# Two recurrences of a metaformer on two groups of 256 columns instead of four of 128

## The chip, the cores and the metric

The kernel runs on one core of one Trainium2 chip. The metric is device time in microseconds of one execution. Before the change the median of three runs is 1061.53 us (1059.64 to 1063.08). All data are 32-bit floats.

## The reference, cut to what matters

The network is two layers. In each, a token mixer (an attention block in layer 0, a filtered convolution with up- and down-sampling in layer 1) is followed by a recurrent feed-forward part, and the two recurrent parts are what the change is about. `x` has 4 batches of 32 tokens, each an image of 128 rows by 128 columns. The recurrent part sees every image row as one time step with 128 features, over 128 sequences (4 batches x 32 tokens). What is computed is:

```python
def _L0_ffn_ref(x, W, V, gamma, beta):      # _L1_ffn_ref is the same
    Wx = jnp.einsum('bti,hi->bth', x, W)
    flat = Wx.reshape(B * T, H)
    mean = jnp.mean(flat, axis=0)
    var = jnp.var(flat, axis=0)
    Wx = ((flat - mean) * jax.lax.rsqrt(var + BN_EPS) * gamma + beta).reshape(B, T, H)
    Vt = V.T

    def step(yt, wx_t):
        yt = jax.nn.sigmoid(wx_t + yt @ Vt)
        return (yt, yt)
    y0 = jnp.zeros((B, H), dtype=Wx.dtype)
    _, ys = jax.lax.scan(step, y0, jnp.swapaxes(Wx, 0, 1))
    return jnp.swapaxes(ys, 0, 1)
```

The sequence of a batch runs through all its tokens' rows, 32 x 128 = 4096 steps, each of which needs the state that the step before left. The result is added to the input of the part.

## The kernel before, in words

**How the long sequence becomes short ones.** The constants are `P = 128`, `NB = 4` batches, `NT = 32` tokens, `LEN = 32`, `WARM = 12` and `QS = P // LEN = 4`. Each image of 128 rows is cut into 4 segments of 32 rows, and all 32 x 4 images run at once. A segment doesn't know the state with which it begins. So each starts 12 rows early from a guess of 0.5 (the warm-up), and the state it has reached by then is used as the true one. After the main pass of 32 rows, `check` compares every segment's true last state with the warm-up's state of its follower. If any pair differs by over 4e-6 in absolute terms, the whole network is run again by a serial version (`sequential`); the runs here don't take that path.

**One step.** The products `W x` of a layer lie in `WX`, a view `[128 features, 4 groups of 8 tokens, 128 rows, 32]` of the tile `WXY`; the 32 is 8 tokens x 4 batches. `step(q, dst, prev, h)` (L1708) does one row `h` of one segment `q`, 128 columns (4 groups x 32 images): a product with `V` on PE into a PSUM bank of the segment's own, `ps_scan` (L1712); the combine with the row of `WX`, scaled by the normalisation, on DVE in place in PSUM (L1713); and the sigmoid on ACT into `dst` (L1714). A product is two passes on PE, so two LDWEIGHTS and two MATMUL instructions.

**Who waits for whom.** Inside a segment the three steps form a chain: the product of row i+1 needs the sigmoid of row i. The four segments are independent of each other, and their steps are traced in turn, segment by segment inside a row. `scan` (L1692) runs 12 warm-up rows and then 32 main rows this way, 44 x 4 = 176 steps per layer and 352 in all. At the end of the warm-up, the state of the last segment (`last`) is copied to the next token's first segment, `G[:, 0]`, shifted by four columns (L1729); the start of the very first token is zero (the memset in L1703).

**The two calls.** In the first layer `f0.scan()` writes each main row's state over its own row of `WX`; the convolution then reads it from there through `rows` (L1762), four PE transposes into `ps_y` for each token and an addition on DVE (L1796). In the second layer `f1.scan(output)` puts each row's state in a tile `y` of its own, two buffers for each segment, and after the steps of row i calls `output(i - 1)` (L1930): four PE transposes of the row before (L1937), one DVE addition of 512 columns to the image rows (L1938), and after every second row four stores of 128 KB on SyncE's queue.

**What sets the order.** Nobody writes the order of the engines by hand here: a scheduler orders the traced instructions by the order in which they were traced and by when their operands and buffers are ready. It also adds the waits. The mixers ahead of the recurrence have their order written out (`MIXERS`, `in_order`), which stays as it is.

**What lies around.** Ahead of the first recurrence, the last products of layer 0 go into `WX`; then the normalisation's scale and shift `s` are made by DVE and POOL (L1695 to L1700). After it comes the convolution, then the products of layer 1, the second recurrence with its output, and the checks.

Of the kernel before, what the change touches and what calls it, by code (L numbers as in the profile page):

```python
# [26 lines left out]
F32 = mybir.dt.float32  # L27
AF = mybir.ActivationFunctionType
ALU = mybir.AluOpType
# [3 lines left out]
P = 128  # L33
NB, NT = 4, 32
# [9 lines left out]
LEN, WARM = 32, 12  # L44
QS = P // LEN
# [149 lines left out]
def _network(  # L195
# [14 lines left out]
    nc = tc.nc  # L210
    mm = nc.tensor.matmul
    tt = nc.vector.tensor_tensor
    stt = nc.vector.scalar_tensor_tensor
# [4 lines left out]
    first = l0.enter_context(tc.tile_pool(name="first", bufs=1))  # L218
# [7 lines left out]
    WX = WXY[:, : 4 * P * TP * NB].rearrange("p (o h n) -> p o h n", o=4, h=P)  # L226
# [43 lines left out]
    def sm(shape, tag):  # L270
        return small.tile(shape, F32, tag=tag, name=tag)


    def rsqrt(o, v, eps, n):

        e = sm([P, NG], "rs_e")[:, :n]
        nc.vector.tensor_scalar_add(e, v, eps)  # L277
        nc.gpsimd.tensor_tensor(o, e, neg_half[:, :n], ALU.pow)  # L278
# [199 lines left out]
    def big(name):  # L478
        return psb.tile([P, 512], F32, tag="big", name=name)
# [233 lines left out]
    with (  # L713
# [168 lines left out]
        p = big("ps_s4")[:, :NB]  # L882
# [23 lines left out]
        for b in range(NB):  # L906
            q = slice(32 * b, 32 * b + 32)
            nc.scalar.copy(gram[q, :], pg[q, 32 * (b % 2) : 32 * (b % 2) + 32])
        p = big("ps_sl")[:, :NT]
# [20 lines left out]
        p = big("ps_pt").rearrange("p (g n) -> p g n", g=4)  # L930
# [17 lines left out]
        for b in range(NB):  # L948
            q = slice(32 * b, 32 * b + 32)
# [52 lines left out]
    with (  # L1002
# [3 lines left out]
        ys = [psy.tile([P, 8, 2 * KW], F32, name=f"ps_y{k}") for k in range(4)]  # L1006
        for g in range(4):
            for x_ in range(2):
# [13 lines left out]
                for k in range(4):  # L1022
                    r, half = divmod(k, 2)
                    m = slice(2 * KW * half, 2 * KW * (half + 1))

                    for b in range(NB):
                        c = slice(32 * b, 32 * b + 32)
                        i = mm(ys[k][c], PTs[:, 1 if (x_ == 1 and r == 0) else 0, g, c],  # L1028
                               df[b][:, r ^ x_, :, m], start=(g == 0 and x_ == 0), stop=(g == 3 and x_ == 1))
                        if k + b > 0:  # L1030
                            tc.keep_in_program_order(i)
        for k in range(4):
            r, half = divmod(k, 2)
            dst = YT[:, r, 16 * half : 16 * half + 16, :KW].rearrange("p (j k) w -> p k j w", k=8)
# [8 lines left out]
    with (  # L1043
# [9 lines left out]
        def one(name):  # L1053
            return np_.tile([P, 1], F32, name=name)
# [6 lines left out]
        def besides(n):  # L1061
# [3 lines left out]
        var, v0, r1, s, a, e1, q1, sv, s0 = (  # L1065
            one(k) for k in ("var", "v0", "r1", "s", "a", "e1", "q1", "sv", "s0"))
# [38 lines left out]
        p = ps3.tile([P, 1], F32, tag="e2", name="ps_e2")  # L1105
# [24 lines left out]
        for v, dst in ((a, aB), (r1, r1B)):  # L1130
            d = np_.tile([P, P], F32, tag="dg", name="dg")
            ts(d, ident, v, None, ALU.mult)
            p = ps3.tile([P, P], F32, tag="dg", name="ps_dg")
# [4 lines left out]
        p = ps3.tile([P, NT], F32, tag="dq", name="ps_dq")  # L1138
# [7 lines left out]
    with (  # L1146
# [16 lines left out]
        chunks = NT // TM  # L1163
        Z, SQ, Fz, G, gB, xin = {}, {}, {}, {}, {}, {}

# [12 lines left out]
        last = chunks - 1  # L1178

        def here(d, c, pool_, shape, tag):  # L1180
            if c not in d:
                d[c] = pool_.tile(shape, F32, tag=tag, name=tag)
            return d[c]
# [117 lines left out]
        def PG(c, k):  # L1301

            here(G, c, m2, [P, TM, 3, KH], "G3")
            g1, g2 = (m1.tile([P, TM, KH], F32, tag=t, name=t) for t in ("g1", "g2"))
# [3 lines left out]
            pool(g2, wi, Fz[c][:, i], ALU.mult)  # L1308
            pool(G[c][:, :, int(k)], g1, g2, o)

# [42 lines left out]
        def M4b(c, k):  # L1353
            Gc = G[c][:, :, 1:3]
            tt(Gc, Gc, vec["al"].unsqueeze(2).unsqueeze(3).broadcast_to([P, TM, 2, KH]), ALU.mult)
            stt(Gc, Y3[:, 1:3, :, of_tokens(c)].rearrange("p r k t -> p t r k"), scalar("attn_norm_g"), Gc,
                ALU.mult, ALU.add)

        def M4c(c, k):
            tt(G[c][:, :, 1, 16], G[c][:, :, 1, 16], vec["de"], ALU.add)  # L1360
            ts(G[c][:, :, 0], G[c][:, :, 2], -1.0, None, ALU.mult)

# [119 lines left out]
        with in_order():  # L1482
            for piece in MIXERS.split():
                name, c = piece.split(".")
                work = shared if inputs is None else shared | features
                f = max((n for n in shared | features if name.startswith(n)), key=len)
# [174 lines left out]
    def parallel():  # L1661
# [9 lines left out]
        xtp = ctx.enter_context(tc.tile_pool(name="xtp", bufs=1))  # L1671
        wk = ctx.enter_context(tc.tile_pool(name="wk", bufs=2))
# [6 lines left out]
        rest = WXY[:, 4 * P * TP * NB :]  # L1679
        guess = xtp.tile([P, NT * NB], F32, name="guess")  # L1680
        nc.gpsimd.memset(guess, 0.5)

        class Recurrence(Inputs):
# [8 lines left out]
            def scan(self, after=None):  # L1692

                mv = xtp.tile([P, 2], F32, name=f"mv{self.layer}")
                nc.vector.bn_aggr(mv, self.stats.rearrange("p t s -> p (t s)"))  # L1695
                s = xtp.tile([P, 2], F32, name=f"bs{self.layer}")
                rsqrt(s[:, 0:1], mv[:, 1:2], 1e-5, 1)
                tt(s[:, 0:1], s[:, 0:1], self.gamma, ALU.mult)
                stt(s[:, 1:2], mv[:, 0:1], -1.0, s[:, 0:1], ALU.mult, ALU.mult)
                tt(s[:, 1:2], s[:, 1:2], self.beta, ALU.add)  # L1700

                G = rest[:, 1024 : 1024 + QS * P].rearrange("p (q n) -> p q n", q=QS)
                nc.gpsimd.memset(G[:, 0, 0:NB], 0.0)  # L1703
                last = xtp.tile([P, NT * NB], F32, name="last")
                ys = {}
                with tc.tile_pool(name="ps_s", bufs=1, space=PSUM) as ps_s:

                    def step(q, dst, prev, h):  # L1708

                        p = ps_s.tile([P, 512], F32, tag=f"s{q}", name=f"ps_scan{q}")[:, :P]  # L1710
                        p4 = p.rearrange("p (o n) -> p o n", o=4)
                        mm(p4, self.t[:, 1, :], prev, start=True, stop=True)  # L1712
                        stt(p4, WX[:, :, h, :], s[:, 0:1], p4, ALU.mult, ALU.add)  # L1713
                        nc.scalar.activation(dst, p4, AF.Sigmoid, bias=s[:, 1:2])  # L1714
                        return dst

                    def tokens(v):
                        return v.rearrange("p (o n) -> p o n", o=4)

                    prev = [tokens(guess)] * QS  # L1720
                    for k in range(WARM):
                        for q in range(QS):

                            if k == WARM - 1:
                                dst = G[:, q] if q else last
                            else:
                                dst = wk.tile([P, NT * NB], F32, tag=f"yw{q}", name=f"yw{q}")
                            prev[q] = step(q, tokens(dst), prev[q], (q * LEN - WARM + k) % P)
                    nc.vector.tensor_copy(G[:, 0, NB:], last[:, : (NT - 1) * NB])  # L1729
                    prev[0] = tokens(G[:, 0])  # L1730
                    for i in range(LEN):
                        for q in range(QS):
                            h = q * LEN + i
                            if after is None:
                                y = WX[:, :, h, :]
                            else:
                                y = wk.tile([P, NT * NB], F32, tag=f"y{q}", name=f"y{q}")
                                ys[q, i] = y
                                y = tokens(y)
                            prev[q] = step(q, y, prev[q], h)  # L1740
                        if after is not None and i > 0:
                            after(i - 1, [ys.pop((q, i - 1)) for q in range(QS)])
                    if after is not None:
                        after(LEN - 1, [ys.pop((q, LEN - 1)) for q in range(QS)])
                self.ends = last, G, prev

            def check(self):
# [33 lines left out]
        with (  # L1781
# [106 lines left out]
            for n in sizes:  # L1888
                last = 2 * t0 - 4
# [7 lines left out]
            for n in sizes[::-1]:  # L1897
                last = 2 * (t0 + n - 1) + 5
# [50 lines left out]
        with tc.tile_pool(name="ps_c", bufs=1, space=PSUM) as ps_c:  # L1949
            p = ps_c.tile([1, 4], F32, name="ps_ok")  # L1950
            mm(p, ones_col, ok, start=True, stop=True)
            n = sm([1, 1], "n_ok")
# [113 lines left out]
```

## Time and profile before

| what | value |
|---|---|
| median of three runs | 1061.53 us |
| the profiled execution, own time | 1060.68 us |
| its span in the profile | 1058.9 us |
| mean granted TensorE clock | 0.947 |
| first recurrence, first combine to last row's first combine | 505.77 to 563.55 us |
| second recurrence, the same | 978.36 to 1046.69 us |
| its main pass begins | 996.24 us |
| combines (L1713), DVE | 352 x 360 ns, 102.2 us |
| products (L1712), PE | two passes each, median 275 ns a pass |
| sigmoids (L1714), ACT | 352, about 363 ns each |

A row of the profile's group table gives the line, the engine and the operation, what is written and read, the shapes as partitions x elements, the count, the total busy time and the mean of one in ns, then the idle time just before and who ended it. A row of the timeline gives the start in us, the length of the merged group, and in brackets the engine's idle time before it and the releaser. PEld is the loading of weights, PE the product itself. DVE and ACT instructions overlap at their edges, so four of 355 ns can take 1.13 us together.

### The profile page before, as it was taken

The page shows a single profiled execution, that of the slowest core. Times are in us where ns is not written, and L with a number is a line of the kernel's source. Part 1 is how long each engine was busy: PE and PEld are TensorE (multiplying, and loading weights), DVE is VectorE, ACT ScalarE, POOL GpSimd, SP SyncE. Part 2 cuts the span into 40 slices and gives each one's busy share as a digit, 9 for nine tenths or more (in the row PEclk, how much of TensorE's full clock was granted, in tenths as well). Part 3 has the DMA queues.
Part 4 walks back from the last instruction along what each step waited for, and adds up shares of the span by engine and source line. Part 5 has one row for each costly group of instructions (what it writes and reads, how often), then busy time and mean ns, then how long its engine had stood idle before and what let it go on. Part 6 is the DMA issues. An engine that isn't in the chain of part 4 may idle for free.

```text
span 1058.9 us, 18079 instructions
## 1 busy us (share of the span) xinstructions
PE 948.9 (90%) x6398; PEld 680.2 (64%) x6398; DVE 775.9 (73%) x2512; ACT 666.6 (63%) x1605; POOL 167.7 (16%) x291
## 2 busy tenths in 40 slices
PE   3999779966889998987898999999999999998996
PEld 2565455655655556543785777777777777775884
DVE  5996387784588899988888656666657566556997
ACT  3767355664637789978784545565546465655864
POOL 1000000010343535552000111111120202010000
PEclk9999989996668899999998999999999999999898
DMA  9723000001011111210000000000100000104644
GB/s 230 174 37 74 1 1 1 1 1 40 2 41 40 41 42 41 61 41 1 1 1 1 20 22 21 20 21 21 31 20 21 20 21 21 30 21 135 227 162 138
DMA packets 68965, 48.83 MB, mean 46 GB/s; under 512 B 4417, under 2 KB 63809, under 8 KB 68801
## 3 DMA queue, kind: packets, MB, share of 16 engines
q1 hardware_dynamic: 68529, 47.31, 15.5%
q8 instruction: 53, 0.87, 0.4%
q0 software_dynamic: 288, 0.01, 0.2%
q10 hardware_dynamic: 48, 0.26, 0.1%
q14 instruction: 47, 0.39, 0.1%
HBM read 30.68 MB, written 16.88 MB: 45 GB/s over the span
## 4 chain that ended last, share of the span: by engine, by line
PE 55%; DVE 23%; ACT 11%; POOL 6%; issue 3%; DMA 1%; SPq 0%; POOLq 0%; ACTq 0%; DVEq 0%
PE ps_up L1854 8%; PE ps_scan L1712 7%; PE ps_dn L1866 7%; PE ps_dn L1875 3%; PE ps_up L1843 3%; DVE XA L1382 3%; PE ps_wx L362 3%; PE ps_st L1224 3%; PE ps_st L765 3%; PE ps_y L1028 2%; DVE XA L1381 2%; PE ps_inv L397 2%; PE pm L970 2%; POOL c_r L278 2%; DVE ps_scan L1713 2%
## 5 line engine op out<-in xcount | busy, mean ns | idle before, releaser
L1857 DVE SCALAR_TENSOR_TENSOR U<-ps_up,above 128x512 f32<-128x512 f32 x128 | 86.7, 690 | 89.9 <-ACT above L1856 89.8
L1854 PE MATMUL ps_up<-q,WXY 128*128 128x512 f32 x256 | 124.0, 606 | 6.0 <-ACT q L1846 6.0
L1866 PEld LDWEIGHTS ps_dn<-WXY,U 128*128 128x128 f32 x1024 | 124.4, 192 | 3.3
L1866 PE MATMUL ps_dn<-WXY,U 128*128 128x128 f32 x1024 | 124.6, 275 | 0.0
L1713 DVE SCALAR_TENSOR_TENSOR ps_scan<-WXY,bs,ps_scan 128x128 f32<-128x128 f32 x352 | 102.2, 360 | 11.4 <-PE ps_scan L1712 10.0
L1856 ACT ACTIVATE above<-ps_up 128x512 f32<-128x512 f32 x128 | 74.4, 596 | 24.6 <-PE ps_up L1854 24.6
L1868 ACT COPY q<-ps_dn 128x512 f32<-128x512 f32 x64 | 37.5, 586 | 71.9 <-PE ps_dn L1866 71.9
L362 PE MATMUL ps_wx<-xt,wvt 128*128 128x512 f32 x128 | 69.0, 625 | 6.3 <-ACT WXY L369 4.0
L1843 PEld LDWEIGHTS ps_up<-WXY,XN 128*128 128x128 f32 x256 | 49.1, 192 | 34.8 <-issue 15.9
L1854 PEld LDWEIGHTS ps_up<-q,WXY 128*128 128x128 f32 x256 | 44.0, 193 | 38.9 <-issue 23.9
L278 POOL TENSOR_TENSOR f_r<-rs_e,neg_half 128x16 f32<-128x16 f32 (+2 forms) x10 | 23.9, 2394 | 278.4 <-DVE rs_e L277 278.4
L1843 PE MATMUL ps_up<-WXY,XN 128*128 128x256 f32 x256 | 66.6, 383 | 0.5 <-DVE XN L1813 0.5
L1875 PE MATMUL ps_dn<-q,WXY 128*128 128x256 f32 x256 | 66.0, 380 | 0.0
L765 PE MATMUL ps_st<-cst,XA 128*128 128x130 f32 x256 | 44.2, 312 | 15.0 <-ACT XA L748 12.0
L1218 ACT ACTIVATE Z<-Z,k,aB 128x128 f32<-128x128 f32 x128 | 51.3, 483 | 9.8 <-DVE Z L1213 9.8
L1875 PEld LDWEIGHTS ps_dn<-q,WXY 128*128 128x128 f32 x256 | 46.1, 190 | 16.4 <-issue 12.0
L1381 DVE SCALAR_TENSOR_TENSOR XA<-ps_inv,r1B,xin 128x128 f32<-128x128 f32 x128 | 44.1, 344 | 13.2 <-PE ps_inv L1374 13.2
L765 PEld LDWEIGHTS ps_st<-cst,XA 128*128 128x128 f32 x256 | 35.6, 208 | 28.2 <-ACT XA L748 13.1
L369 ACT COPY WXY<-ps_wx 128x512 f32<-128x512 f32 x60 | 35.0, 583 | 29.1 <-DVE bn L365 27.8
L1439 ACT ACTIVATE xn<-XA,f_o,f_r 128x128 f32<-128x128 f32 x120 | 50.4, 487 | 2.2 <-DVE f_o L1421 2.2
L412 PE MATMUL ps_inv<-invq,cst 64*128 64x512 f32 x128 | 44.7, 723 | 5.6 <-ACT invq L403 3.3
L1815 ACT ACTIVATE XN<-XA,c_o,c_r 128x128 f32<-128x128 f32 x64 | 28.8, 490 | 32.3 <-DVE c_o L1804 26.3
(425 smaller groups left out, 2143.5 us busy)
## 6 DMA issues: line engine op xcount, KB each, us to landing
XA<-in_x_dram SPq DMA_DIRECT2D x16, 512.0 KB, 7.1
xin<-in_x_dram SPq DMA_DIRECT2D x32, 256.0 KB, 3.3
turned<-XA SPq DMA_DIRECT2D x32, 256.0 KB, 2.3
XA<-turned SPq DMA_DIRECT2D x8, 1024.0 KB, 15.2
out_dram<-res SPq DMA_DIRECT2D x64, 128.0 KB, 2.1
WXY<-dd SPq DMA_DIRECT2D x4, 544.0 KB, 10.7
WXY<-md SPq DMA_DIRECT2D x4, 144.0 KB, 5.3
WXY<-m1d SPq DMA_DIRECT2D x1, 544.0 KB, 11.1
```

The source lines that it names most:

```text
L362: mm(self.held[t], self.t[:, 0, :], xt, start=True, stop=True)
L765: mm(p[:, i, :], XA[:, b, t0 + j + i, :], cst[:, C_E : C_E + 130], start=True, stop=True)
L1218: nc.scalar.activation(z, z, AF.Gelu, bias=k1, scale=aB[:, j : j + 1])
L1381: stt(a, p2[c, b][:, i], r1B[:, j : j + 1], xin[c, b - b % 2][:, b % 2, i], ALU.mult, ALU.add)
L1712: mm(p4, self.t[:, 1, :], prev, start=True, stop=True)
L1713: stt(p4, WX[:, :, h, :], s[:, 0:1], p4, ALU.mult, ALU.add)
L1843: mm(p[:, b, :], XN[u // 2][:, (u % 2) * H2 + b, :], UR.rearrange("p r q -> p (r q)"), start=True, stop=True)
L1854: mm(p, UC[:, s, :], q, start=True, stop=True)
L1856: nc.scalar.activation(above, p, AF.Relu, scale=1.0 - SLOPE)
L1857: stt(U[:, s], p, SLOPE, above, ALU.mult, ALU.add)
L1866: mm(p[:, r, b, :], U[:, s, b, r * P : (r + 1) * P], DC[:, s, :], start=(s == 0), stop=(s == 1))
L1875: mm(p, DR[:, r, :], q[:, r], start=(r == 0), stop=(r == 1))
```

## The change

A step now takes all four segments at once, for half of the tokens: the two groups are `j = 0` (token groups 0 and 1) and `j = 1` (token groups 2 and 3), each 2 x 4 x 32 = 256 columns. Both layers, warm-up and main pass, use the same form. So a row has two products, two combines and two sigmoids of 256 columns in place of four of each of 128.

The warm-up is turned by one place to make this possible. All segments read the row `LEN - WARM + k` of their own segment, and the state that segment q reaches is the beginning of segment q+1; the last warm-up row therefore writes into `ends[:, 1:]`, which is `G[1:]` followed by `last`. `last` moves from a tile of its own to a slice of `WXY` behind `G`. The copy into `G[:, 0]` stands where it stood; `G` is now read by both groups. The states of the warm-up and of the second layer's main pass lie in one tile `y` of 4 x 128 columns with two buffers, in which the halves of the tokens alternate: a group is 4 runs of 64 columns. `output` and `check` get the same values as views of these tiles.

```diff
-                    def step(q, dst, prev, h):
-                        p = ps_s.tile([P, 512], F32, tag=f"s{q}", name=f"ps_scan{q}")[:, :P]
-                        p4 = p.rearrange("p (o n) -> p o n", o=4)
-                        mm(p4, self.t[:, 1, :], prev, start=True, stop=True)
-                        stt(p4, WX[:, :, h, :], s[:, 0:1], p4, ALU.mult, ALU.add)
-                        nc.scalar.activation(dst, p4, AF.Sigmoid, bias=s[:, 1:2])
-                        return dst
+                    def step(dst, prev, i):
+                        for j in range(2):
+                            p = ps_s.tile([P, 512], F32, tag=f"s{j}", name=f"ps_scan{j}")[:, : 2 * P]
+                            p4 = p.rearrange("p (o q n) -> p o q n", o=2, q=QS)
+                            mm(p4, self.t[:, 1, :], prev(j), start=True, stop=True)
+                            v = p.rearrange("p (m n) -> p m n", n=32)
+                            stt(v, rows_in[:, i, 2 * QS * j : 2 * QS * (j + 1)], s[:, 0:1], v, ALU.mult, ALU.add)
+                            nc.scalar.activation(dst(j), p4, AF.Sigmoid, bias=s[:, 1:2])
...
                     for k in range(WARM):
-                        for q in range(QS):
...
-                            prev[q] = step(q, tokens(dst), prev[q], (q * LEN - WARM + k) % P)
+                        dst = images(ends[:, 1:] if k == WARM - 1 else wk.tile([P, QS, P], F32, tag="y", name="y"))
+                        step(dst, prev, LEN - WARM + k)
+                        prev = dst
                     nc.vector.tensor_copy(G[:, 0, NB:], last[:, : (NT - 1) * NB])
-                    prev[0] = tokens(G[:, 0])
+                    prev = images(G)
                     for i in range(LEN):
-                        for q in range(QS):
...
-                            prev[q] = step(q, y, prev[q], h)
+                        y = None if after is None else wk.tile([P, QS, P], F32, tag="y", name="y")
+                        dst = at_row(i) if after is None else images(y)
+                        step(dst, prev, i)
                         if after is not None and i > 0:
-                            after(i - 1, [ys.pop((q, i - 1)) for q in range(QS)])
+                            after(i - 1, [y0[:, q] for q in range(QS)])
+                        prev, y0 = dst, y
```

The new helpers choose the columns of a group: `half` takes 4 runs of 64 out of 4 images of 128, `at_row` takes 2 x 4 x 32 out of `WX`, and `first` spreads the guess over the segments.

```diff
+                ends = rest[:, 1024 : 1024 + (QS + 1) * P].rearrange("p (q n) -> p q n", n=P)
+                G, last = ends[:, :QS], ends[:, QS]
...
+                rows_in = WX.rearrange("p o (q i) n -> p i (o q) n", q=QS)
...
+                def half(v, j):
+                    return v.rearrange("p q (o n) -> p o q n", o=4)[:, 2 * j : 2 * j + 2]
...
+                    def at_row(i):
+                        return lambda j: WX.rearrange("p o (q i) n -> p i o q n", q=QS)[:, i, 2 * j : 2 * j + 2]
+
+                    def first(j):
+                        return tokens(guess)[:, 2 * j : 2 * j + 2].unsqueeze(2).broadcast_to([P, 2, QS, 32])
```

## The prediction

> **What bounds the kernel now.** I read the page first, then the windows of the two recurrences, then the timeline of a few rows, then the waits. The page shows an execution in which PE looks full and the combine of the recurrence (L1713) is the costliest vector group:
>
> ```profile
> span 1058.9 us, 18079 instructions
> PE 948.9 (90%) x6398; PEld 680.2 (64%) x6398; DVE 775.9 (73%) x2512; ACT 666.6 (63%) x1605; POOL 167.7 (16%) x291
> ...
> L1713 DVE SCALAR_TENSOR_TENSOR ps_scan<-WXY,bs,ps_scan 128x128 f32<-128x128 f32 x352 | 102.2, 360 | 11.4 <-PE ps_scan L1712 10.0
> ```
>
> The change touches only the two recurrences, so I read those stretches. The windows' columns are busy times of PE, PEld, DVE, ACT, POOL, then granted clock, DMA share, GB/s:
>
> ```profile
> 489.00:500.00 11.00, 7.17 (x29) 3.23 (x28) 10.00 (x37) 9.16 (x20) 1.66 (x2) 1.00 0.00 1
> 521.00:567.00 46.00, 41.83 (x267) 35.34 (x266) 39.22 (x139) 37.62 (x132) 0.10 (x1) 1.00 0.00 1
> 980.00:985.00 5.00, 5.00 (x26) 5.00 (x25) 4.11 (x12) 3.90 (x12) 0.00 (x0) 0.50 1.05 397
> 996.00:1049.00 53.00, 51.38 (x384) 43.46 (x383) 52.53 (x161) 36.98 (x129) 0.00 (x0) 1.00 0.41 141
> ```
>
> The second row is the first recurrence's main pass: no engine is full. The fourth is the second recurrence's: DVE works 52.53 of 53 us. The timeline shows why they differ. One row of the first recurrence:
>
> ```profile
> 523.43 1.13 DVE L1713 SCALAR_TENSOR_TENSOR ps_scan<-WXY,bs,ps_scan 128x128 f32<-128x128 f32 x4 [0.21 <-PE ps_scan L1712]
> 523.82 1.14 ACT L1714 ACTIVATE WXY<-ps_scan,bs 128x128 f32<-128x128 f32 x4 [0.20 <-DVE ps_scan L1713]
> 524.24 1.07 PEld L1712 LDWEIGHTS ps_scan<-WXY,wvt 128*128 128x128 f32 x8 [0.27 <-ACT WXY L1714]
> 524.76 1.13 DVE L1713 SCALAR_TENSOR_TENSOR ps_scan<-WXY,bs,ps_scan 128x128 f32<-128x128 f32 x4 [0.21 <-PE ps_scan L1712]
> ```
>
> Four segments pass in a convoy. The lead one goes DVE to ACT in 0.39 us, ACT to PE in 0.42, PE to the next DVE in 0.52: together 1.33 us, exactly the row's period, and every engine idles 0.20 to 0.27 us before the lead. So a row here costs the **latency of one chain**, not work: DVE's four combines take 1.13 us, the period is 1.33. In the second recurrence's main pass DVE also has the output addition:
>
> ```profile
> 1001.07 1.12 DVE L1713 SCALAR_TENSOR_TENSOR ps_scan<-WXY,bs,ps_scan 128x128 f32<-128x128 f32 x4
> 1002.10 0.68 DVE L1938 TENSOR_TENSOR res<-XA,ps_out 128x512 f32<-128x512 f32 x1
> 1002.70 1.13 DVE L1713 SCALAR_TENSOR_TENSOR ps_scan<-WXY,bs,ps_scan 128x128 f32<-128x128 f32 x4
> ```
>
> Here the row is 1002.70 - 1001.07 = 1.63 us = 1.03 for four combines + 0.60 for the addition: **DVE work** bounds it, above the 1.33 us latency. The waits (total us, times, longest) agree: DVE waits for PE 43 times in the first recurrence,
>
> ```profile
> DVE ps_scan L1713 <- PE ps_scan L1712: 9.0, 43, 0.3
> ```
>
> and in the second's main stretch twice, while ACT waits for DVE in every row:
>
> ```profile
> ACT y L1714 <- DVE ps_scan L1713: 15.3, 32, 0.6
> ...
> DVE ps_scan L1713 <- PE ps_scan L1712: 0.5, 2, 0.3
> ```
>
> [...] This trace: 411 ns at 256 columns and 704 at 512 (rows below), 1.14 ns an element; 683 at 512 in L1796 gives 1.06. [...] Trace: 262 ns at 130 columns, 368 at 256, 0.84 per column. [...] the sigmoid of 128 columns took 362. [...] Here a 128-column pass of L1712 has a median of 275 ns and a 256-column one a mean of 383, so 0.84 ns a column[...], and each product is issued as two passes; I take the measurement, and about 107 ns per pass of 128.
>
> ```profile
> L1843 PE MATMUL ps_up<-WXY,XN 128*128 128x256 f32 x256 | 66.6, 383 | 0.5 <-DVE XN L1813 0.5
> ...
> L1877 DVE TENSOR_TENSOR XA<-XA,ps_dn 128x256 f32<-128x256 f32 x64 | 26.3, 411 | 3.7 <-PE ps_dn L1875 1.9
> L1938 DVE TENSOR_TENSOR res<-XA,ps_out 128x512 f32<-128x512 f32 x32 | 22.5, 704 | 0.0
> ...
> L1236 ACT COPY Fz<-ps_pf 128x256 f32<-128x256 f32 x8 | 2.9, 368 | 5.4 <-PE ps_pf L384 5.3
> ...
> L769 ACT COPY A<-ps_st 128x130 f32<-128x130 f32 x8 | 2.1, 262 | 0.3 <-PE ps_st L765 0.3
> ```
>
> **The change, part by part.**
>
> *Two instructions of 256 columns for four of 128.* Work falls. On DVE one combine follows another after 0.26 us ((1.13 - 0.355)/3), so a row goes from 1.03 to 2 x (0.26 + 0.133) = 0.79 us; ACT likewise to 2 x (0.26 + 0.107) = 0.73. PE streams the same columns. But each chain gets longer, because no engine starts before the one ahead has finished its whole instruction (ACT starts 0.39 after a 0.355 us combine). The lead chain's growth: DVE +133 ns, ACT +107 ns, PE two passes of +107 = +213 ns, in all **+0.453 us**. The row becomes 1.335 + 0.453 = **1.788 us**, against 0.79 us of DVE and 0.73 of ACT work: latency-bound again, the halves following each other by about 0.43 us (PE's own time for a product).
>
> *First recurrence.* The lead combines of its 44 rows run from 505.77 to 563.55: 43 intervals, 57.78 us. One interval is special: the step from warm-up to main takes 1.60, since the copy of `last` into `G` (L1729) stands ahead of segment 0. After, both halves read the copied image, and the copy shifts by four columns across the halves, so it needs both sigmoids: 0.43 lag + 0.22 copy + 0.09 hand-overs = 0.74 extra where 0.27 was. Sum: 43 x 1.788 + 0.74 = 77.6, +19.8 us. The last chain trails the lead by 0.43 rather than 3 x 0.26 = 0.78: -0.35. **+19.5 us.**
>
> *Second recurrence, warm-up.* It runs from 978.36 to 996.24, 17.88 us. Here the clock was 0.50 for about 6.8 us (window means 0.84, 0.50 and 0.98 over 975 to 990), with 12 combines in 5 us, so 1.67 us a row: 0.33 over the full-clock row, three passes' worth (one weight load and two products of 107 ns). After, that streaming is 0.107 + 0.427 = 0.53, and a half-clock row 1.788 + 0.53 = 2.32. So 6.8/2.32 = 2.9 rows, then 9.1 x 1.788 = 16.2, plus 0.74: 23.8 us. **+5.9 us.** I keep the same half-clock time[...].
>
> *Second recurrence, main.* 31 intervals took 1046.69 - 996.24 = 50.45. DVE work is now 0.79 + 0.60 = 1.39, below the latency; PE has 0.86 of products and 4 x 0.11 of transposes, 1.3. The addition must sit between the second half's combine (free 0.82 us after the lead starts) and the next lead at 1.788: 0.97 us of room for 0.60. The transposes of the row before follow the second product in PE's queue and end before the lead's next product. So 31 x 1.788 = 55.4, +5.0, less 0.26 of shorter trail. **+4.7 us.**
>
> *The rest at nothing, together.* The row order is the same, `y` keeps two buffers, memset, check and DMAs are as before: the output stores move 8.4 MB in 57 rather than 52 us, and POOL has one memset. Were the stores' cover gone, each lands in 2.1 us, once, at the end. 176 fewer instructions each on DVE and ACT shorten no path by themselves.
>
> Sum: 19.5 + 5.9 + 4.7 = +30.1 on the profiled execution's 1060.68 (span 1058.9 and 1.8 around it), 0.85 under the median: 1090.8, so **1091**.
>
> **Unknown costs.** No row shows a combine, a sigmoid or a product with this 8 x 32 pattern at 256 columns. [...] a pattern of more, shorter runs may cost some more (today's 4 x 32 takes 355 ns in L1713, a contiguous one 344 in L1381), say 0.02. Over 87 rows: -0.5 to +3 us. Below nothing is excluded, as each instruction streams twice the columns. The slot of the addition and transposes isn't shown: nothing if they fit, up to 0.3 us a row (31 rows, +9) if not. The half-clock time may vanish (-1.5) or double (+1.5). The step into the main pass may hide behind DVE's gaps (-1 for both). The three runs shown lie 1059.64 to 1063.08, so 2 us either way.
>
> **Rivals.** (a) *The transposes come late*: with two buffers of `y`, the sigmoid of row i+1 waits for the transposes of row i-1. If these are queued behind the second product of row i+1, the lead's sigmoid waits 0.3 us: 31 x 0.3, 1100 us. For it: the engine order is the scheduler's, and transposes already interleave with products today. Against: they are ready a row earlier. (b) *The change isn't what it says*: both halves lie interleaved in one tile, and if a product waits for the sigmoid of the other half the two chains run in lockstep: +0.43 a row, at 56 rows (warm-ups and second main) to 87: 1115 to 1128. Against: now four segments interleave just so in `WX` and don't wait for each other. (c) *PE cools*: its passes fill about 48% of a row rather than 64%; at half clock throughout a row is 2.32: 1091 + 75 x 0.53 = 1131. Against: the first window above, where 9 passes of 512 columns and 20 of 128 in 11 us (at 0.84 ns a column 6.0 us, 55% at most) keep the clock at 1.00. (d) **Faster**: work sets the pace, not latency. The second main stretch does follow DVE work today; if halving fixed costs carried through and the longer instructions hardly lengthened a chain, that stretch would fall to its latency, 31 x 1.335 = 41.4 (-9), with the rest unchanged: 1053. It decides from the growth of a row: 87 d - 9 + 1 < 0, so under 0.09 us instead of 0.453. Against: the legs of the lead chain add up to its period with no queueing left in it.
>
> **How the numbers follow.** Forecast 0.75; (a) 0.12; (b) 0.06; (c) 0.03; (d) 0.03; nearly no change, by parts I don't see, 0.01. The range takes forecast and (a) with their unknowns: 1086 to 1103. Within 0.3% (3 us) is about what a measurement can tell from none: faster 0.03, same 0.01, slower 0.96.
>
> **What would show it.** Right: 176 combines near 490 ns and sigmoids near 470; lead combines 1.79 us apart in both main stretches; DVE idle waiting for PE in the second as well, where it isn't now. Wrong: a period above 2 us in the second main stretch only (a), in nearly all rows at full clock (b), with PEclk near 0.5 (c), or combines 256 wide and rows no longer than 1.4 us (d).

## The result and the profile after

The changed kernel takes 1100.61 us (median; its runs lie from 1090.17 to 1100.86) against 1061.65 for the kernel before beside it: the ratio is 1.033, interval 1.0268 to 1.0393, so it is slower by 39 us. The same kernel, in five further runs (experiment 1), takes 1093.95 us against 1063.08, ratio 1.0297 (1.0271 to 1.0323), slower by 31 us. The forecast was 1091, that is 30 us more.

The profiled execution took 1100.86 us, with a span of 1099.0 and a mean granted clock of 0.933, where the kernel before had 0.947. Here are the engines' row of its page and the group table's rows for combine and sigmoid:

```profile
PE 959.3 (87%) x6046; PEld 655.1 (60%) x6046; DVE 760.6 (69%) x2336; ACT 643.8 (59%) x1429; POOL 167.7 (15%) x291
...
L1722 DVE SCALAR_TENSOR_TENSOR ps_scan<-WXY,bs,ps_scan 128x256 f32<-128x256 f32 x176 | 82.5, 489 | 57.5 <-PE ps_scan L1720 57.5
...
L1723 ACT ACTIVATE y<-ps_scan,bs 128x256 f32<-128x256 f32 x108 | 49.7, 473 | 53.6 <-DVE ps_scan L1722 51.5
```

DVE and ACT do less than before: 760.6 us instead of 775.9, and 643.8 instead of 666.6. The combines alone fell from 102.2 to 82.5 us, while the time that DVE stands idle ahead of them, waiting for the product, rose from 11.4 to 57.5. Less work and a longer span is the mark of a chain that got longer. The timeline of two rows in the first recurrence's main pass shows its legs:

```profile
538.97 0.92 DVE L1722 SCALAR_TENSOR_TENSOR ps_scan<-WXY,bs,ps_scan 128x256 f32<-128x256 f32 x2 [0.86 <-PE ps_scan L1720]
539.49 0.91 ACT L1723 ACTIVATE WXY<-ps_scan,bs 128x256 f32<-128x256 f32 x2 [0.88 <-DVE ps_scan L1722]
540.01 0.73 PEld L1720 LDWEIGHTS ps_scan<-WXY,wvt 128*128 128x128 f32 x4 [1.06 <-ACT WXY L1723]
...
540.75 0.92 DVE L1722 SCALAR_TENSOR_TENSOR ps_scan<-WXY,bs,ps_scan 128x256 f32<-128x256 f32 x2 [0.86 <-PE ps_scan L1720]
```

DVE to ACT takes 0.52 us (it was 0.39), ACT to PE 0.52 (0.42), PE to the next DVE 0.74 (0.52): 1.78 us a row, where it was 1.33. DVE and ACT wait nearly 0.9 us for the lead half, PE 0.65. In the second recurrence's main pass the output addition (L1947) and the transposes (L1946) lie in the gaps of the same row:

```profile
1061.23 0.92 DVE L1722 SCALAR_TENSOR_TENSOR ps_scan<-WXY,bs,ps_scan 128x256 f32<-128x256 f32 x2 [0.23 <-PE ps_scan L1720]
...
1061.46 0.60 PE L1946 MATMUL ps_out<-ident,y 128*128 128x128 f32 x4
...
1062.10 0.69 DVE L1947 TENSOR_TENSOR res<-XA,ps_out 128x512 f32<-128x512 f32 x1
...
1063.02 0.92 DVE L1722 SCALAR_TENSOR_TENSOR ps_scan<-WXY,bs,ps_scan 128x256 f32<-128x256 f32 x2 [0.23 <-PE ps_scan L1720]
```

The row is 1063.02 - 1061.23 = 1.79 us. Before the lead combine DVE is now idle for 0.23 us and released by PE; in the kernel before it followed the addition without a gap. The list of waits over this stretch agrees: DVE waits for PE 32 times there, 8.6 us in all, where it was twice and 0.5.

**Where the 40.1 us of span went.** The times of the first combine, of the main pass's start and of the last row's lead combine divide the two profiled executions:

| stretch | before | after | difference | forecast |
|---|---|---|---|---|
| up to the first combine | 505.77 | 512.95 | +7.2 | 0 |
| first recurrence, warm-up | 16.3 | 24.2 | +7.9 | |
| first recurrence, main pass | 41.5 | 55.4 | +13.9 | |
| both together | 57.8 | 79.6 | +21.9 | +19.8 |
| from its end to the second recurrence | 414.8 | 414.7 | -0.1 | -0.35 |
| second recurrence, warm-up | 17.9 | 23.6 | +5.7 | +5.9 |
| second recurrence, main pass | 50.45 | 55.4 | +5.0 | +5.0 |
| from its last row's lead to the end | | | +0.5 | -0.3 |

The recurrences thus cost 32.6 us more where 30.7 were forecast. The 7.2 us ahead of the first combine lie in work that the change doesn't touch. A window of that work in the changed kernel (columns: busy us of PE, PEld, DVE, ACT, POOL, then granted clock, DMA share, GB/s):

```profile
300.00:500.00 200.00, 186.50 (x1552) 112.85 (x1550) 170.95 (x602) 155.24 (x415) 87.82 (x202) 0.84 0.13 38
```

The clock is 0.84; in the kernel before it was 0.91 over the same 200 us, and DVE got through 627 instructions and ACT through 428 there, against 602 and 415 here. Whether that belongs to the change or to the execution needs the same kernel again.

### The profile page after: what moved, and what is told of

The parts are those of the page before. It is cut to its first block, busy times and chain, and to the rows that moved or that the text cites. A ratio compares the mean times of both kernels' runs of the same rounds, so it can differ in the third digit from the quotient of the medians.

```text
span 1099.0 us, 17011 instructions
## 1 busy us (share of the span) xinstructions
PE 959.3 (87%) x6046; PEld 655.1 (60%) x6046; DVE 760.6 (69%) x2336; ACT 643.8 (59%) x1429; POOL 167.7 (15%) x291
## 4 chain that ended last, share of the span: by engine, by line
PE 54%; DVE 24%; ACT 12%; POOL 4%; issue 3%; DMA 1%; SPq 0%; POOLq 0%; ACTq 0%; DVEq 0%
PE ps_up L1863 8%; PE ps_dn L1875 7%; PE ps_scan L1720 6%; DVE ps_scan L1722 4%; PE ps_dn L1884 3%; PE ps_up L1852 3%; PE ps_wx L362 3%; PE ps_st L1224 3%; DVE XA L1382 3%; PE ps_inv L397 3%; PE ps_st L765 2%; ACT y L1723 2%; PE ps_y L1028 2%; DVE XA L1381 2%; PE pm L970 2%
## 5 line engine op out<-in xcount | busy, mean ns | idle before, releaser
L1722 DVE SCALAR_TENSOR_TENSOR ps_scan<-WXY,bs,ps_scan 128x256 f32<-128x256 f32 x176 | 82.5, 489 | 57.5 <-PE ps_scan L1720 57.5
L1720 PE MATMUL ps_scan<-y,wvt 128*128 128x256 f32 x212 | 69.2, 439 | 17.2 <-ACT y L1723 16.7
L1723 ACT ACTIVATE y<-ps_scan,bs 128x256 f32<-128x256 f32 x108 | 49.7, 473 | 53.6 <-DVE ps_scan L1722 51.5
L362 PE MATMUL ps_wx<-xt,wvt 128*128 128x512 f32 x128 | 72.3, 652 | 5.9 <-ACT WXY L369 3.6
L1852 PEld LDWEIGHTS ps_up<-WXY,XN 128*128 128x128 f32 x256 | 49.2, 193 | 34.5 <-issue 16.3
L1720 PEld LDWEIGHTS ps_scan<-y,wvt 128*128 128x128 f32 x212 | 33.9, 200 | 47.9 <-ACT y L1723 43.3
L1720 PE MATMUL ps_scan<-WXY,wvt 128*128 128x256 f32 x132 | 37.4, 406 | 23.1 <-ACT WXY L1723 20.3
L1884 PEld LDWEIGHTS ps_dn<-q,WXY 128*128 128x128 f32 x256 | 46.1, 190 | 16.3 <-issue 12.0
## 6 DMA issues: line engine op xcount, KB each, us to landing
WXY<-dd SPq DMA_DIRECT2D x4, 544.0 KB, 10.7
```

The lines of the kernel that those rows point to most:

```text
L362: mm(self.held[t], self.t[:, 0, :], xt, start=True, stop=True)
L1720: mm(p4, self.t[:, 1, :], prev(j), start=True, stop=True)
L1722: stt(v, rows_in[:, i, 2 * QS * j : 2 * QS * (j + 1)], s[:, 0:1], v, ALU.mult, ALU.add)
L1723: nc.scalar.activation(dst(j), p4, AF.Sigmoid, bias=s[:, 1:2])
L1852: mm(p[:, b, :], XN[u // 2][:, (u % 2) * H2 + b, :], UR.rearrange("p r q -> p (r q)"), start=True, stop=True)
L1884: mm(p, DR[:, r, :], q[:, r], start=(r == 0), stop=(r == 1))
```

## The experiments

Two theories stood against each other at first. The **chain** theory (L in the expectations): a row costs the sum of the legs of one group's chain, each leg grows with the group's columns, and the number of groups is free. The **form** theory (G): it is the new form (turned warm-up, shared tiles, runs of 32 columns) or a wait between groups that costs. Later came a third question, how much **PE's clock** adds (P). C is the rival by which the change itself, and not the clock, costs the 9 us above the forecast; W is the rival by which an engine's work sets the pace.

**1. The changed kernel once more**, without an edit, for the 7.2 us.

> The changed kernel once more, unaltered. Theory L (the growth of the row is chain latency; the 9 us above the forecast are half-clock time of PE, most of it ahead of the recurrences where the program is the same): the times fall into two groups, near 1091 us when the mean granted clock is 0.95 and near 1100 us when it is 0.93, and the rows of both recurrences are 1.79 us in either. Rival C (the change itself costs the 9 us): all times near 1100 us and the 1090.17 us run was the odd one.

Measured: 1093.95 us (1093.59 to 1100.54), ratio 1.0297 (1.0271 to 1.0323). Its first combine stands at 506.51 us, and its window ahead of the recurrence has the clock and very nearly the counts of the kernel before:

```profile
300.00:500.00 200.00, 180.71 (x1565) 105.47 (x1565) 177.14 (x628) 160.59 (x426) 90.77 (x205) 0.91 0.13 38
```

So the 7.2 us came with that execution, not with the change. The kernel of experiment 4 with the new form in its first recurrence also has its first combine at 505.68 us. The times of single runs follow their mean clock: 1100.5 us at 0.933, 1093.6 at 0.945, and 1090.2 at 0.951 in the first comparison. But this execution lost time inside the recurrences instead. Windows at the start of the first one and around its step into the main pass:

```profile
507.00:512.00 5.00, 3.78 (x9) 2.01 (x10) 2.35 (x6) 2.27 (x5) 0.00 (x0) 0.63 0.00 0
534.00:540.00 6.00, 5.25 (x11) 2.30 (x10) 2.53 (x7) 2.80 (x6) 0.00 (x0) 0.58 0.00 0
```

Over the rest of that main pass the clock was 1.00. PE fell to half clock at 508 us for 10.2 us and at 532 for 6.8, and twice more for 6.8 us in the second recurrence, at 1006.7 and at 1027.1. Behind the last, the lead combines start at 1028.54 and 1030.85 us, a row of 2.31. Its recurrences together took 163.2 us, against 158.6 in the first profile and 126.1 in the kernel before. So rival (c), PE at half clock, had a part of the truth: not throughout, but for a few rows at the starts and after a step.

**2. Four groups of 128 columns, in the changed form.** Everything of the change stays, the halves become quarters of the tokens; the other slices of two groups follow likewise.

```diff
-                    return v.rearrange("p q (o n) -> p o q n", o=4)[:, 2 * j : 2 * j + 2]
+                    return v.rearrange("p q (o n) -> p o q n", o=4)[:, 1 * j : 1 * j + 1]
...
-                        for j in range(2):
-                            p = ps_s.tile([P, 512], F32, tag=f"s{j}", name=f"ps_scan{j}")[:, : 2 * P]
-                            p4 = p.rearrange("p (o q n) -> p o q n", o=2, q=QS)
+                        for j in range(4):
+                            p = ps_s.tile([P, 512], F32, tag=f"s{j}", name=f"ps_scan{j}")[:, : 1 * P]
+                            p4 = p.rearrange("p (o q n) -> p o q n", o=1, q=QS)
```

> The new form with four groups of 128 columns, each a quarter of the tokens with all segments; all else as in the changed kernel. Theory L: what counts is the columns of an instruction, so rows are back at 1.34 us in the first recurrence and 1.63 in the second's main pass; the step into the main pass is some 0.8 us longer than before, as the copy now needs all four sigmoids: 1063 us, plus up to 10 if PE falls to half clock ahead of the recurrence. Rival G (the new grouping, with its 32-column runs, the shared tile of states and the copy, is what costs): rows stay at 1.6 us or more in the first recurrence and the time at 1080 us or above.

Measured: 1064.54 us (1061.71 to 1071.87) against 1063.08, ratio 1.0019 (0.9991 to 1.0046). The first recurrence's rows are back at 547.17 - 545.84 = 1.33 us:

```profile
545.84 1.13 DVE L1722 SCALAR_TENSOR_TENSOR ps_scan<-WXY,bs,ps_scan 128x128 f32<-128x128 f32 x4 [0.21 <-PE ps_scan L1720]
547.17 1.13 DVE L1722 SCALAR_TENSOR_TENSOR ps_scan<-WXY,bs,ps_scan 128x128 f32<-128x128 f32 x4 [0.21 <-PE ps_scan L1720]
```

In the second main pass they take 1.63 us, as in the kernel before. The form theory falls: turned warm-up, shared tiles and runs of 32 columns cost 1.5 us by the medians and at most 4.9 by the interval (0.0046 x 1063). 0.8 us of it shows in the first recurrence's step into the main pass, 2.38 us instead of 1.60, and 1.0 in the second's, 2.62 instead of 1.64, since there the copy waits for all four groups. The grouping by 256 columns is the cause. With 512 columns in all, a group's width and the number of groups change together, and no run here separates them; that it is the width is read from the legs, which grew by 0.13, 0.10 and 0.22 us, about what their own instructions grew.

**3. One group of 512 columns.** If a leg grows by a fixed amount per column, one group gives 1.335 + 3 x 0.453 = 2.69 us a row; if two groups were slow because one hinders the other, one alone would be faster than two.

```diff
-                    return v.rearrange("p q (o n) -> p o q n", o=4)[:, 2 * j : 2 * j + 2]
+                    return v.rearrange("p q (o n) -> p o q n", o=4)[:, 4 * j : 4 * j + 4]
...
-                        for j in range(2):
-                            p = ps_s.tile([P, 512], F32, tag=f"s{j}", name=f"ps_scan{j}")[:, : 2 * P]
-                            p4 = p.rearrange("p (o q n) -> p o q n", o=2, q=QS)
+                        for j in range(1):
+                            p = ps_s.tile([P, 512], F32, tag=f"s{j}", name=f"ps_scan{j}")[:, : 4 * P]
+                            p4 = p.rearrange("p (o q n) -> p o q n", o=4, q=QS)
```

> One group of all 512 columns in both recurrences, one look. Theory L: the row is the chain's latency and grows by a fixed amount per column, 3.5 ns, so 1.335 + 0.40 (combine) + 0.32 (sigmoid) + 0.64 (product) = 2.69 us in both main passes at full clock; the step into the main pass costs only the copy, 0.3 us more. Sum +107 us, so about 1170 us. PE's passes fill only 32% of such a row; if that lets the clock fall to half, a row takes 3.66 us and the time goes up to 1250. Rival W (work sets the pace): the work of a row falls once more, DVE to 0.79 us less two fixed parts, and the row is at most the 1.79 us of the changed kernel: about 1090 us.

Measured: 1232.73 us, in a single run, against a median of 1065.29 for the kernel before on that chip. Two lead combines of its second main pass, with the addition wholly in the gap, on DVE's timeline:

```profile
1180.21 0.75 DVE L1722 SCALAR_TENSOR_TENSOR ps_scan<-WXY,bs,ps_scan 128x512 f32<-128x512 f32 x1 [1.35 <-PE ps_scan L1720]
1180.87 0.68 DVE L1947 TENSOR_TENSOR res<-XA,ps_out 128x512 f32<-128x512 f32 x1
1182.90 0.76 DVE L1722 SCALAR_TENSOR_TENSOR ps_scan<-WXY,bs,ps_scan 128x512 f32<-128x512 f32 x1 [1.35 <-PE ps_scan L1720]
```

That is 2.69 us at full clock. So 128, 256 and 512 columns give 1.335, 1.788 and 2.69 us: 3.54 ns per column, on a line. The time lies at the half-clock end of what was expected: at half clock a row took 3.64 us, and PE stayed there for the 149 us of this window, nearly all of the first recurrence (clock 0.50):

```profile
513.00:662.00 149.00, 85.07 (x82) 20.62 (x82) 30.58 (x42) 28.17 (x41) 0.10 (x1) 0.50 0.00 0
```

Its two recurrences take 294.1 us together, 168.0 more than before, and that is the whole difference (167.4).

**4. The change in one recurrence only.** Both forms of `scan` stand in the kernel, and each recurrence calls one.

```diff
-        f0.scan()
+        f0.scan_new()
...
-            f1.scan(output)
+            f1.scan_old(output)
```

> Only the first recurrence in the new form, the second as before. Theory L: +19.5 us by the rows (44 of 1.79 against 1.34 us), so 1081 us, up to 1091 with half-clock time; the second's main rows 1.63 us. Rival C: 1090 us in every run.

Measured: 1081.82 us (1079.55 to 1084.3), ratio 1.0179 (1.0152 to 1.0206), +18.7 us. The two forms in one execution, from the group table:

```profile
L1777 DVE SCALAR_TENSOR_TENSOR ps_scan<-WXY,bs,ps_scan 128x128 f32<-128x128 f32 x176 | 50.9, 344 | 2.5 <-PE ps_scan L1776 1.0
...
L1722 DVE SCALAR_TENSOR_TENSOR ps_scan<-WXY,bs,ps_scan 128x256 f32<-128x256 f32 x88 | 41.2, 488 | 37.6 <-PE ps_scan L1720 37.6
```

Half as many combines need 41.2 us of DVE instead of 50.9, and DVE waits 37.6 us ahead of them.

The other way round:

```diff
-        f0.scan()
+        f0.scan_old()
...
-            f1.scan(output)
+            f1.scan_new(output)
```

> Only the second recurrence in the new form, the first as before. Theory L: +10.6 us (+5.9 in the warm-up, +4.7 in the main pass), so 1072 us, up to 1080 with half-clock time; first recurrence rows 1.34 us, main rows of the second 1.79. Rival C (the 9 us belong to the new form of the first recurrence): always 1072 us.

Measured: 1071.99 us (1069.09 to 1075.59), ratio 1.0088 (1.0057 to 1.0118), +8.9 us. The two parts give 18.7 + 8.9 = 27.6 us, the whole change 30.9 in the same comparison. With intervals of about 3 us to either side for each, the sum holds. The two profiles say the same: the first recurrence takes 20.9 us more in one, the second 10.7 in the other. The second of these runs alone decides nothing, as both L and C put it at 1072 us; the first does, against C's 1090.

**5. PE kept busy.** The chain theory says that PE's gaps are free to fill, and the clock question can be asked with them: one more product of 256 columns, into a PSUM bank that nobody reads, in each row in which no transposes stand.

```diff
-                    def step(dst, prev, i):
+                    def step(dst, prev, i, fill):
...
+                        for _ in range(fill):
+                            p = ps_s.tile([P, 512], F32, tag="fill", name="ps_fill")[:, : 2 * P]
+                            mm(p.rearrange("p (o q n) -> p o q n", o=2, q=QS), self.t[:, 1, :], prev(1), start=True, stop=True)
...
-                        step(dst, prev, LEN - WARM + k)
+                        step(dst, prev, LEN - WARM + k, 3 if k == WARM - 1 else 1)
...
-                        step(dst, prev, i)
+                        step(dst, prev, i, 1 if after is None else 0)
```

> The changed kernel with one product more of 256 columns per row, whose result nobody reads, behind the second product in the first recurrence and both warm-ups (three at the last warm-up row); PE then fills 72% of a row instead of 48%. Theory P (the new form leaves PE so idle that its clock falls to half in and around the recurrences, some 2 to 6 us in a run): no half-clock time inside the recurrences but that at the second's start, rows of 1.79 us from the first row on, and a median below that of the changed kernel's repeat, 1089 to 1092 against 1094 us. If the half-clock time stems only from the stages ahead, the time is that of the changed kernel, 1093 to 1100 us. If the filler stands in the products' way, rows grow to 2.0 us and the time to 1105.

Measured: 1094.72 us (1091.45 to 1097.05) against 1065.29, ratio 1.0276 (1.0252 to 1.03), +29.4 us. So the median that theory P expected, 1089 to 1092 us, was missed, while its rows came out as it said. The added product (L1726) fits between the second half's product and the next lead without moving a row, which is 542.02 - 540.23 = 1.79 us:

```profile
540.23 0.92 DVE L1722 SCALAR_TENSOR_TENSOR ps_scan<-WXY,bs,ps_scan 128x256 f32<-128x256 f32 x2 [0.87 <-PE ps_scan L1720]
...
540.46 0.59 PE L1726 MATMUL ps_fill<-WXY,wvt 128*128 128x256 f32 x2
...
542.02 0.92 DVE L1722 SCALAR_TENSOR_TENSOR ps_scan<-WXY,bs,ps_scan 128x256 f32<-128x256 f32 x2 [0.87 <-PE ps_scan L1720]
```

Its window over the first recurrence's main pass is at full clock, and so are both warm-ups:

```profile
531.00:584.00 53.00, 46.42 (x180) 28.96 (x178) 27.52 (x60) 26.55 (x59) 0.00 (x0) 1.00 0.00 1
```

Its recurrences take 156.0 us, +29.9 on the 126.1 of the kernel before, against 158.6 and 163.2 in the two profiles of the changed kernel. So the half-clock rows are worth about 2.6 and 7.2 us in those two executions, as an estimate from these sums. The times don't show it: +29.4 against +30.9 us, with intervals of about 3 us to either side. The clock ahead of the recurrences alone varies enough from one execution to another to cover it, as the 7.2 us above show.

**6. The work that bounds the second main pass, taken off the kernel before.** If that pass follows DVE's work at 128 columns, less work on DVE there should pay, where wider groups do not. Half of the output addition goes to POOL, by way of a copy out of PSUM that ACT makes.

```diff
-                tt(res[:, :, i % 2, :], XA[:, :, i, :], p, ALU.add)
+                tt(res[:, :2, i % 2, :], XA[:, :2, i, :], p[:, :2], ALU.add)
+                c = outp.tile([P, 2, P], F32, name="rest_out")
+                nc.scalar.copy(c, p[:, 2:])
+                nc.gpsimd.tensor_tensor(res[:, 2:, i % 2, :], XA[:, 2:, i, :], c, ALU.add)
```

> The kernel before, four groups of 128; only the output addition of the second recurrence is divided: DVE adds two of the four images, ACT copies the other two out of PSUM and POOL adds them. Theory L says that this main pass is bound by DVE's work (1.03 + 0.60 us a row) and would be bound by latency, 1.34 us, if DVE had less: DVE 1.03 + 0.33, ACT 1.03 + 0.28, so rows of about 1.40 us instead of 1.63, 31 x 0.23 = 7 us off: 1055 us against 1062. If the copy stands in ACT's queue ahead of a sigmoid of the chain, rows stay near 1.6 us and the time where it was.

Measured: 1061.11 us (1054.68 to 1067.61) against 1065.29, ratio 0.9964 (0.9951 to 0.9977), 4.2 us less: a small gain, but with an interval clear of 1, and about half of the 7 us that were expected. The runs' mean clocks are alike (median 0.938 in both), and the second main pass takes 46.6 us instead of 50.5. On DVE's timeline:

```profile
1019.49 1.19 DVE L1713 SCALAR_TENSOR_TENSOR ps_scan<-WXY,bs,ps_scan 128x128 f32<-128x128 f32 x4
1020.59 0.41 DVE L1938 TENSOR_TENSOR res<-XA,ps_out 128x256 f32<-128x256 f32 x1
1020.92 1.32 DVE L1713 SCALAR_TENSOR_TENSOR ps_scan<-WXY,bs,ps_scan 128x128 f32<-128x128 f32 x4
...
1022.53 1.14 DVE L1713 SCALAR_TENSOR_TENSOR ps_scan<-WXY,bs,ps_scan 128x128 f32<-128x128 f32 x4
```

The addition is down to 0.33 us of DVE's pace (1020.92 - 1020.59). But the rows take 1.43 and 1.61 us in turn, 1.50 in the mean of the pass, where 1.40 was expected. In this stretch no engine but POOL is idle:

```profile
1000.00:1045.00 45.00, 44.46 (x360) 40.59 (x360) 44.86 (x150) 43.98 (x150) 21.02 (x29) 1.00 0.46 161
```

ACT's copy of 373 ns stands between the sigmoids of two rows and takes about 0.27 us of ACT's pace. Whether it is this that holds back every second row was not tried.

## Why the prediction was right, and where it was off

**The bound now: right.** That the first recurrence follows one chain's latency is shown from both sides: widening the groups costs 0.45 us a row (experiments 2 and 3), and in the changed kernel filling PE's gaps costs an ordinary row nothing (5). That the second's main pass follows DVE's work is shown by the 3.8 us that lighter DVE work saves there (6), though the rows got 0.12 us shorter for the 0.27 us taken off DVE, and not the 0.23 expected.

**The growth of a chain: right.** The forecast was 0.133 on DVE, 0.107 on ACT and 0.213 on PE, 1.788 us a row; measured are 1.787 in both main passes, and 2.69 at 512 columns. The instructions came out as taken: the combine 489 ns (about 490), the sigmoid 473 (about 470). The 133 ns on DVE was the author's assumption: the additions of the kernel before, 411 ns at 256 columns and 704 at 512, give 1.14 ns a column and so 146 ns for 128. Measured, the combine grew by 134 ns, from 355 to 489, and by 267 more to 756 at 512 columns; from the mean of 347 ns in the four quarters of experiment 2 it is 142. The new pattern of 8 x 32 columns cost nothing that shows.

**First recurrence: +19.8 forecast from the first lead combine to the last, +21.9 measured.** Two terms were too small. One is "the step into the main pass", 2.53 us by the working (1.788 + 0.74), 2.90 measured. The timeline of that step:

```profile
534.28 0.49 DVE L1722 SCALAR_TENSOR_TENSOR ps_scan<-WXY,bs,ps_scan 128x256 f32<-128x256 f32 x1 [0.45 <-PE ps_scan L1720]
...
535.13 0.49 DVE L1722 SCALAR_TENSOR_TENSOR ps_scan<-WXY,bs,ps_scan 128x256 f32<-128x256 f32 x1 [0.36 <-PE ps_scan L1720]
...
536.16 0.23 DVE L1740 COPY WXY<-WXY 128x124 f32<-128x124 f32 x1 [0.54 <-ACT WXY L1723]
...
537.18 0.92 DVE L1722 SCALAR_TENSOR_TENSOR ps_scan<-WXY,bs,ps_scan 128x256 f32<-128x256 f32 x2 [0.79 <-PE ps_scan L1720]
```

The second half trails the lead by 535.13 - 534.28 = 0.85 us, not by the 0.43 that the working took. The halves started the recurrence at half clock, and there their combines stood 0.86 us apart (515.36 and 516.22 us), twice the 0.43 of the working; at full clock nothing moved them together again until both waited for the copy (L1740). In the kernel with filled gaps, whose clock didn't fall there, they stay 0.43 apart up to the copy. 0.85 + 0.53 to ACT + 0.50 to the copy + 1.02 from the copy to the combine = 2.90 us. The other is the half clock itself: none was assumed for this recurrence, and its first three rows took 2.3 to 2.4 us, 1.7 us more in all.

**Second recurrence: right**, +5.7 for the warm-up (forecast +5.9) and +5.0 for the main pass (forecast +5.0). The warm-up's sum is so close partly by luck: a row at half clock took 2.31 us for the 2.32 that had been worked out, but for two rows rather than 2.9 (0.5 us less), and the step into the main pass took 2.87 us instead of 2.53 (0.3 more). The working took over the half-clock time of the kernel before. It isn't set by the stretch ahead alone: the kernel with filled gaps has a clock of 1.00 over 1000 to 1021 us, behind the same stretch.

**The rest at nothing: within a microsecond.** From the last row to the end 0.5 us were added, where 0.3 less was forecast. The 7.2 us ahead of the first combine were the execution's and not the change's.

**The rivals.** (a), late transposes, did not occur: they run right behind the second product (1061.46 in the timeline above), and the row is 1.79. That the first comparison's median, 1100.6 us, is (a)'s number is chance. (b), coupled halves, did not occur: four quarters in the same tiles run at 1.33 us. (c), PE at half clock, came true in small: 2.6 and 7.2 us in two executions, not throughout; only with one group of 512 columns did it last (0.50 over 513 to 662 us). (d), work as the pace, is refuted by the rows of all three widths.

**What stays open** is why PE's clock falls more in one execution than in another ahead of the first recurrence. The instructions are the same there, but the clock over 300 to 500 us was 0.84 in one execution of the changed kernel and 0.91 in the other, and 0.88 to 0.93 in the other kernels. No run here separates a cause. For the recurrences themselves the last section goes further.

## What to carry to other kernels

Where every step needs the step before, ask first whether a row costs one chain's legs or an engine's work: the timeline tells, by an engine that idles ahead of the lead group or one that never does. Wider instructions took the combines' work here from 102.2 to 82.5 us, and in the first case that gained nothing (the first recurrence took 21.9 us more): there every column was paid once per engine of the chain, 3.5 ns in all where the wider DVE instruction alone pays 1.05. From this it follows, though only one, two and four groups were tried, that the right number of groups is the one at which the busiest engine's work in a row just reaches the legs' sum; beyond that, move work off that engine.

## What was not expected of the hardware

PE's clock in a chain with gaps. By an estimate from 0.84 ns a column and pass (passes of 275 ns at 128 columns and 383 at 256), the products stream for about 48% of a row at 256 columns (0.86 of 1.79 us). The busy time in the windows is larger than that: the same rows count as 64% busy (33.02 of the 52 us from 540 us on). The clock was 1.00 there, but at starts and steps of the two executions of the changed kernel it fell to half for 6.8 to 10.2 us. With the added product (by the same estimate 1.28 of 1.79 us, 72%) it never fell inside a recurrence: it was 1.00 over 507 to 528, 529 to 585, 1000 to 1021 and 1024 to 1077 us. With one group of 512 columns (0.86 of 2.69 us, 32%) it stayed at 0.50 over 513 to 662 us in the first recurrence and at 0.51 over 1083 to 1166 in the second, and then at 1.00 over 1166 to 1215.

A single pause of PE doesn't tell where the clock falls. In the first execution of the changed kernel PE paused for 2.06 us up to 514.10 us, and the clock fell at 514.04; in the second the longest pause ahead of the drop at 532 us was 1.35 us. In the first, a pause of the same 1.35 us up to 536.44 us had no drop behind it (clock 1.00 over 537 to 540 us).

In the traces of the kernel before and of the first execution of the changed kernel, the 25 and the 31 changes of the clock lie whole multiples of 3.413 us apart, to within 2 ns, and this grid begins at another place in each, 2.20 us after the start of the span in the one and 2.04 in the other. So the same thin stretch of work can be cut in another way each time. These are the 3.41 us that end with the drop at 532 us in the second execution, and the interval of the grid that holds the same step into the main pass in the first:

```profile
528.80:532.21 3.41, 1.51 (x6) 0.68 (x4) 1.69 (x5) 1.37 (x3) 0.10 (x1) 1.00 0.02 5
...
534.52:537.93 3.41, 1.71 (x6) 0.85 (x6) 1.71 (x5) 1.18 (x3) 0.10 (x1) 1.00 0.02 5
```

PE is busy for 44% of the one, and at its end the clock falls; for 50% of the other, and no drop comes of it. In the recurrences of the kernel before and of the first execution of the changed kernel, with the 2 us ahead of each, 81 intervals of the grid at full clock end. The three with the least PE busy (1.10, 1.28 and 1.60 us) were followed by half clock, the 78 with 1.71 us or more were not. In the second execution the clock also fell, at 1027.1 us, behind 3.40 us with 1.78 of PE busy. So within these recurrences the drops mostly came behind the intervals in which PE was least full. This is read from the traces and not tried by an experiment, and it isn't the whole of it: ahead of the first recurrence of the kernel before, the clock fell at 360.6 us behind 3.40 us in which PE was busy for 3.13, that is 92%.

The clock is also what single runs differ by: 1090.2 us at a mean of 0.951 and 1100.9 at 0.933 for the same changed kernel, 10.7 us and so a third of the change's effect.
